# A decoder layer on one core: engine orders in the attention loop, roots by logarithm and exponential, and both joints rearranged

## The chip, the core and the metric

The kernel runs on one core of a Trainium2 chip. The core has TensorE (PE: matmuls and transposes, with its weight loads shown apart as PEld), VectorE (DVE), ScalarE (ACT), GpSimd (POOL), and SyncE (SP), which here only issues DMAs. Each engine works through its own instructions in order and waits on semaphores for the others. The metric is the device time of one execution in microseconds. The kernel before takes 967.76 us, the median of three runs (966.3 to 969.13).

## The reference

All of it is float32: 4096 tokens (16 sequences of 256) of width 256. There are three parts, each followed by a layer norm of x plus its result.

```python
# 1: "attention" against 1024 fixed rows, squared relu instead of softmax (4 heads of 64)
p = jnp.square(jax.nn.relu(jnp.einsum('bhtd,sd->bhts', q, k)))     # q from layernorm(x)*g+b
out = residual + jnp.einsum('bhts,sd->bhtd', p, v)
x = _layernorm(x + out)
# 2: cross attention, 16 heads of 16, with a bias from clipped differences of frac
D = jnp.clip(frac[:, None, :] - frac[:, :, None], -0.2, 0.2)
attn = gamma*logits + delta*(alpha_pos*max(D, 0) + alpha_neg*min(D, 0))
x = _layernorm(x + (softmax(attn) @ V) @ Wo.T + bo)
# 3: top-1 of 8 experts, a shared inner matrix plus a rank-4 part of the expert
inter = relu(x @ wi_W.T + wi_b + lora(x, expert))
x = _layernorm(x + inter @ wo_W.T + wo_b)
```

The root that this case is about is the `rsqrt(var + 1e-5)` of the layer norms, one for each row.

## The kernel before

The order of the work is written out by hand (`manual_schedule`): each engine gets its instructions in the order of the program text. There are three stages and two joints between them.

**First stage** (lines 872 to 953): eight blocks of 512 tokens. For each block and each of eight pieces, `scores` multiplies with the fixed rows, ScalarE applies relu, VectorE squares, and `values` accumulates into two banks. `keep` (331) brings these two banks together: ScalarE copies both, GpSimd adds. `turn_out` (337) turns the result back and forms y = 2x + out on VectorE; `measure_out`, `scaling` and `norm_out` give the normalized rows in `hid`. Slots between the pieces hold the clips of the frac differences (`clips`, `slots`, 859 to 863).

**Second stage** (964 to 1036): 64 groups, four for each of 16 sequences (a batch), each group with four heads (g = 0 to 3). Iteration n works on three groups at once. For group n (`now`): `logits` (592), sixteen matmuls on top of the seeds; `maxima` (606) on VectorE, which adds the negative bias, writes t and keeps the row maxima; `subtract` (617), one half on GpSimd and one on VectorE. For group n+1 (`nxt`): `negative` (571, 576) on GpSimd and ScalarE; `positive` (583), the seed, which ScalarE writes into the bank of PSUM that the logits then add to. It can only be written when the maxima have read that bank. For group n-1 (`last`): `turned(g)` (631), four transposes of t, and `exps(g)` (638), the exponential out of PSUM. For group n-2 (`older`): `attend` (647) and `keep` (655), which copies the finished pair of groups to `raw`; after the second pair, `gather` (502) issues nine DMAs, `sums` and eight pieces of `v`.

Beside that, `pieces(n)` (670) hands out a large piece of matmuls by n modulo 4: 0 the next batch's `queries`, 1 the batch-before-last's `project`, 2 the next `keys`, 3 the next `vals`. Each is a generator of two steps: matmuls into a bank of `tile_b`, then the eviction, on VectorE (on ScalarE for queries). `keys` ends with eight DMAs into `kM`, the four of i=0 first; `logits` of the first and third group of a batch read i=0, of the second and fourth i=1. With n modulo 4 = 2 comes `invert` (519): a reciprocal on VectorE, one DMA `rows` to DRAM, then eight DMAs `invs` back, broadcast. With 3 come the transposes of a later batch's hidden rows (`turned`, 409) and its context; with 0 the `divide` (537), which reads `invs`. All these DMAs are issued on SyncE's queue.

`tile_b` (49) gives the banks for transposes and large pieces: in the second and third stage every third tile comes from the pool psV and the others from the two banks of psB, so the same bank comes round every third tile.

**Third stage** (1038 to 1092): for each block of 512 tokens `norm`, `turn` (707), `gates` (720), `route` (735, the expert's mask), `turn_um` (767), `inner` (778), `lora` (796), `outer` (815), `add` and `store` (835).

`inv_std` (194) gives a row's root everywhere: Sqrt on ScalarE, then a reciprocal on VectorE. In the second stage ScalarE's order in an iteration is: `negative`, `positive(0)`, `positive(1)`, `exps(0)`, `positive(2)`, `exps(1)`, `positive(3)`, `exps(2)`, `exps(3)`. VectorE's is: `maxima`, `subtract`, then the evictions.

Of the kernel before, what the change touches and what calls it, by code (L numbers as in the profile page):

```python
# [14 lines left out]
P = 128  # L15
# [6 lines left out]
def tile_decoder_layer(ctx: ExitStack, tc: tile.TileContext, a: dict, out: bass.AP):  # L22
# [62 lines left out]
    root = const.tile([P, 1], FP, name="root")  # L85
    nc.scalar.activation(root, epst, AF.Sqrt)
# [107 lines left out]
    def inv_std(mv, n):  # L194

        sd = small.tile([P, n], FP, tag="sd", name="sd")
        nc.scalar.activation(sd, mv[:, :, 1], AF.Sqrt, bias=epst)
        rs = small.tile([P, n], FP, tag="rs", name="rs")
        nc.vector.reciprocal(rs, sd)
        return rs  # L200
# [25 lines left out]
    if True:  # L226
# [14 lines left out]
        class Block:  # L241
# [89 lines left out]
            def keep(self, c):  # L331
                half = p1.tile([P, 512], FP, tag="half", bufs=1, name="half")
                nc.scalar.copy(self.oT[:, c, :], self.acc[0])
# [3 lines left out]
            def turn_out(self, jj):  # L337
# [3 lines left out]
                for j in range(2):  # L341
                    for c in range(CC):
# [4 lines left out]
                        )  # L347
                nc.vector.scalar_tensor_tensor(
# [23 lines left out]
    if True:  # L372
# [184 lines left out]
        class Group:  # L557
# [59 lines left out]
            def subtract(self):  # L617
                for g, eng in ((0, nc.gpsimd), (2, nc.vector)):
# [36 lines left out]
            def keep(self):  # L655
                batch = self.batch
                if self.i == 1:
                    if self.o == 0:
                        batch.raw = pm.tile([P, 2, 512], FP, tag="raw", name="raw")
                    if self.o == 0:  # L660
                        nc.vector.tensor_copy(batch.raw[:, self.o, :], batch.av)
                    else:
                        nc.scalar.copy(batch.raw[:, self.o, :], batch.av)
                        batch.gather()
# [25 lines left out]
    if True:  # L690
        out_view = out.rearrange("(b j p) c -> b p j c", j=4, p=P)

        class Block:
# [3 lines left out]
            def norm(self):  # L697
                tb = self.tb
                mv = small.tile([P, 4, 2], FP, tag="mv", name="mv")
                for j in range(4):  # L700
                    row_stats(hid[:, 4 * tb + j, :], mv[:, j, :])
                rs = inv_std(mv, 4)
                self.x2 = tile_x()
                for j in range(4):
                    normed(self.x2[:, j, :], hid[:, 4 * tb + j, :], mv[:, j, 0:1], rs[:, j : j + 1])

            def turn(self):
                self.xT = tile_xt()
                for c in range(CC):
# [5 lines left out]
                    nc.vector.tensor_copy(self.xT[:, c, :], ps)  # L715
# [136 lines left out]
    with tc.manual_schedule():  # L852
# [7 lines left out]
        slots = [(1, (5, 6, 7)), *((tb, (0, 3, 5, 6, 7)) for tb in range(2, 5))]  # L860
# [11 lines left out]
        for tb in range(NB):  # L872
# [6 lines left out]
            if tb > 0:  # L879
                last = rows_in[tb - 1]  # L880
                steps[1] += [lambda: last.turn_out(0), lambda: last.turn_out(1)]
# [77 lines left out]
        block.keep(1)  # L959
# [3 lines left out]

        for n in range(N + 2):
# [4 lines left out]
            if n == 0:  # L969
                small_piece = batches[1].turned()  # L970
# [50 lines left out]
            if n == N:  # L1021
                block.gates()
            if n % 4 == 0:
# [143 lines left out]
```

## Time and profile before

| | |
|---|---|
| median of three runs | 967.76 us |
| the profiled execution | 968.68 us, its span 966.9 us |
| first stage, to the first logits | 268.35 us |
| logits of group 8, 60, 63 start | 328.88, 655.17, 674.06 us |
| steady batch of four groups | 24.95 us |
| first `inner` of the third stage starts | 691.59 us |
| block of the third stage, steady | 32.6 us (738.06 to 770.69) |
| busy PE, DVE, ACT, POOL | 911.5, 708.4, 585.3, 413.6 us |
| activation table loads on ACT | 7, 1283 ns each |

Lines of a timeline read: start in us, length in us, engine, line of the kernel, operation, out<-in, the shapes, how many instructions were merged (x8), and in brackets the idle time of the engine before it with what ended that. SPq is SyncE's queue issuing a DMA. A busy PE is not PE at its peak: matmuls are pipelined, and a matmul that is held up shows longer or starts later.

### The profile page before, as it was taken

What the parts mean: (1) busy time and instruction counts of PE and PEld (TensorE: products, weight loads), DVE (VectorE), ACT (ScalarE), POOL (GpSimd) and SP (SyncE); (2) the same over time, 40 slices, a digit from 0 to 9 for tenths busy, and PEclk for the clock granted to TensorE, in tenths of its full rate; (3) what the DMA queues carried; (4) which work ended last, traced back from release to release, by engine and by line L of the source; (5) the groups of instructions that cost most, each with busy time, mean ns of one, the idle gap of its engine ahead of it and who ended that gap; (6) DMA issues with size and microseconds to landing.
All of it is one profiled execution on the core that took longest, in us unless ns stands there. A gap on an engine that the chain in (4) does not pass through costs nothing.

```text
span 966.9 us, 19117 instructions
## 1 busy us (share of the span) xinstructions
PE 911.5 (94%) x6910; PEld 545.7 (56%) x6910; DVE 708.4 (73%) x1909; ACT 585.3 (61%) x956; POOL 413.6 (43%) x352
## 2 busy tenths in 40 slices
PE   5999999999978999999999999998889999999997
PEld 2333333333345676777676777775446656565656
DVE  4789999999877888888889888888543534453424
ACT  4757776778679888999898999998311010101010
POOL 1102211323466787888888888887211101100100
PEclk9999999999989999999999999999989999999999
DMA  6312221122001222222222222221100000000001
GB/s 171 107 39 77 69 66 64 61 67 66 23 1 45 67 51 62 61 65 63 68 64 69 65 68 67 67 65 35 31 5 1 23 22 1 23 22 22 0 22 44
DMA packets 50526, 48.54 MB, mean 50 GB/s; under 512 B 15616, under 2 KB 40704, under 8 KB 50432
## 3 DMA queue, kind: packets, MB, share of 16 engines
q1 hardware_dynamic: 49712, 46.53, 17.0%
q8 instruction: 55, 0.90, 0.4%
q10 hardware_dynamic: 720, 0.79, 0.3%
q14 instruction: 39, 0.32, 0.1%
HBM read 26.84 MB, written 11.80 MB: 40 GB/s over the span
## 4 chain that ended last, share of the span: by engine, by line
PE 52%; DVE 8%; ACT 3%; issue 2%; SPq 1%; DMA 1%; ACTq 0%; DVEq 0%
PE ps_l L788 12%; PE ps_v L818 10%; PE ps_b L631 7%; PE ps_l L592 6%; PE ps_v L647 4%; DVE t L606 3%; DVE t L621 2%; PE ps_b L442 2%; PE ps_b L544 2%; PE ps_l L800 2%; PE ps_b L422 2%; PE ps_b L818 1%; ACT ps_l L583 1%; ACT pT L638 1%; PE ps_b L712 1%
## 5 line engine op out<-in xcount | busy, mean ns | idle before, releaser
L571 POOL TENSOR_SCALAR neg<-dneg,aneg,delta 128x512 f32<-128x512 f32 x192 | 214.0, 1124 | 0.0
L606 DVE CUSTOM_DVE_ANT_0 t<-ps_l,neg 128x256 f32<-128x256 f32 x512 | 181.4, 420 | 40.8 <-PE ps_l L592 34.9
L583 ACT ACTIVATE ps_l<-dpos,apos_d 128x512 f32<-128x512 f32 x256 | 175.9, 693 | 36.4 <-DVE mx L606 23.6
L313 DVE TENSOR_TENSOR pr<-r 128x1024 f32<-128x1024 f32 x128 | 160.7, 1295 | 24.1 <-ACT r L311 23.8
L311 ACT ACTIVATE r<-ps_a 128x1024 f32<-128x1024 f32 x128 | 126.4, 1023 | 68.4 <-PE ps_a L303 42.3
L631 PE MATMUL ps_b<-ident,t 128*128 128x128 f32 x1024 | 144.4, 281 | 13.3 <-ACT pT L638 12.3
L621 POOL TENSOR_TENSOR t<-t,mx 128x1024 f32<-128x1024 f32 x64 | 121.2, 1893 | 80.2 <-DVE mx L606 70.2
L638 ACT ACTIVATE pT<-ps_b 128x512 f32<-128x512 f32 x256 | 144.5, 595 | 3.5 <-PE ps_b L631 2.9
L631 PEld LDWEIGHTS ps_b<-ident,t 128*128 128x128 f32 x1024 | 113.5, 141 | 56.2 <-ACT pT L638 20.5
L323 PE MATMUL ps_v<-pr,vv 64*64 64x512 f32 x1024 | 124.6, 595 | 4.1 <-DVE pr L313 3.6
L303 PE MATMUL ps_a<-xnT,kT 64*64 64x512 f32 x1024 | 123.6, 599 | 0.3 <-ACT r L311 0.3
L788 PE MATMUL ps_l<-xt,wi 128*128 128x512 f32 x256 | 114.6, 601 | 0.0
L621 DVE TENSOR_TENSOR t<-t,mx 128x1024 f32<-128x1024 f32 x64 | 111.9, 1748 | 2.2
L718 POOL TENSOR_TENSOR x<-x,wofb 128x256 f32<-128x256 f32 x32 | 22.7, 739 | 201.2 <-PE ps_b L712 201.2
L818 PE MATMUL ps_v<-wof,hT 128*128 128x256 f32 x448 | 101.4, 383 | 0.0
L807 ACT ACTIVATE hT<-ps_l,wib 128x512 f32<-128x512 f32 x32 | 20.2, 684 | 122.5 <-PE ps_l L800 122.5
L818 PEld LDWEIGHTS ps_v<-wof,hT 128*128 128x128 f32 x448 | 83.7, 190 | 18.8 <-issue 8.4
L335 POOL TENSOR_TENSOR xt<-xt,half 128x512 f32<-128x512 f32 x16 | 24.9, 1558 | 151.1 <-ACT half L334 151.1
L811 DVE TENSOR_SCALAR hT<-ps_l,wib 128x512 f32<-128x512 f32 x32 | 22.5, 746 | 90.2 <-PE ps_l L800 90.2
L323 PEld LDWEIGHTS ps_v<-pr,vv 64*64 64x64 f32 x1024 | 37.2, 132 | 77.9 <-issue 39.7
L788 PEld LDWEIGHTS ps_l<-xt,wi 128*128 128x128 f32 x256 | 48.4, 194 | 54.9 <-issue 54.6
L592 PE MATMUL ps_l<-kM,qT 32*128 32x256 f32 x1024 | 77.0, 406 | 1.2 <-ACT ps_l L583 1.2
(105 smaller groups left out, 1052.2 us busy)
## 6 DMA issues: line engine op xcount, KB each, us to landing
cT<-in_ctxT SPq DMA_DIRECT2D x16, 256.0 KB
kM<-keys SPq DMA_DIRECT2D x128, 32.0 KB
v<-raw SPq DMA_DIRECT2D x128, 32.0 KB
invs<-rows SPq DMA_DIRECT2D x128, 32.0 KB
x<-in_x SPq DMA_DIRECT2D x7, 512.0 KB
away<-dneg SPq DMA_DIRECT2D x14, 256.0 KB
away<-dpos SPq DMA_DIRECT2D x14, 256.0 KB
dneg<-away SPq DMA_DIRECT2D x14, 256.0 KB
```

Of the source, the lines that this page charges most:

```text
L311: nc.scalar.activation(r, sc, AF.Relu)
L313: nc.vector.tensor_tensor(pr, r, r, ALU.mult)
L323: nc.tensor.matmul(self.acc[k][64 * h : 64 * h + 64, :], lhsT=vv[64 * k : 64 * k + 64, hf, 64 * q : 64 * q + 64], rhs=pr[64 * k : 64 * k + ...
L571: nc.gpsimd.tensor_scalar(self.neg[:, g], self.batch.dneg, aneg[:, h : h + 1], delta, ALU.mult, ALU.mult,)
L583: nc.scalar.activation(banks[g], self.batch.dpos.rearrange("p j k -> p (j k)"), AF.Copy, scale=apos_d[:, h : h + 1],)
L592: nc.tensor.matmul(banks[g][:, j * S : (j + 1) * S], lhsT=self.batch.qT[rows, self.o, j * P : (j + 1) * P], rhs=self.batch.kM[rows, self.i ...
L606: nc.vector.tensor_tensor_reduce(out=self.t[:, g, j, :], in0=banks[g][:, j * S : (j + 1) * S], in1=self.neg[:, g, j, :], scale=1.0, scalar ...
L621: eng.tensor_tensor(rows, rows, top.to_broadcast([P, 4, S]), ALU.subtract)
L631: nc.tensor.transpose(ps[:, k * S + j * P : k * S + (j + 1) * P], self.t[:, g, j, k * P : (k + 1) * P], ident,)
L638: nc.scalar.activation(self.pT[:, g, :], self.ps[g], AF.Exp)
L788: nc.tensor.matmul(banks[g], lhsT=wi[:, c, f * P : (f + 1) * P], rhs=self.xT[:, c, :], start=(c == 0), stop=False,)
L818: nc.tensor.matmul(ps[:, at * C : (at + 1) * C], lhsT=self.hT[f][:, j * P : (j + 1) * P], rhs=wof[:, f, :], start=(f == 0), stop=(f == FC ...
```

## The change

- **Roots.** `inv_std` takes Ln and then Exp(-0.5 ln) on ScalarE as a first guess and one Newton step, three small operations, on VectorE. The table set that holds both functions is asked for at the start, instead of a first Sqrt.
- **ScalarE's order** in an iteration of the second stage: all four `positive` come ahead of `exps(1)`.
- **VectorE's order**: `keep` and the second step of the large piece come ahead of `subtract`, except where n modulo 4 is 0 and in iteration 1 (there the second step of the large piece stays behind `exps(3)`). `keep` always copies on VectorE.
- **`invert`** comes ahead of the large piece `keys` of the same iteration.
- **First joint**: the last `keep` of the first stage adds on VectorE out of PSUM; in iteration 0 the transposes of batch 1, `vals` of batch 0 and both `turn_out` are issued between the logits and the maxima, both halves of `subtract` go to GpSimd, `queries` of batch 1 move to iteration 1. The last block's row statistics are taken in iterations 1 to 4, its root in 5, its `norm_out` in 8 to 11.
- **Second joint**: the first block of the third stage is measured in iterations 58 to 61, normalized on ScalarE in 63 (`begin`), turned there with copies on ScalarE, its gates and route taken in iteration 64; after the loop `norm` of the second block follows `inner(0)` and `turn_um` of the first, ahead of `invert` of the last batch.
- One clip in each of three blocks of the first stage moves from piece 3 to piece 0.

```diff
-    root = const.tile([P, 1], FP, name="root")
-    nc.scalar.activation(root, epst, AF.Sqrt)
+    nc.scalar.preload_act_table_set("natural_log_exp_and_others")
...
     def inv_std(mv, n):
 
-        sd = small.tile([P, n], FP, tag="sd", name="sd")
-        nc.scalar.activation(sd, mv[:, :, 1], AF.Sqrt, bias=epst)
+        ln = small.tile([P, n], FP, tag="ln", name="ln")
+        nc.scalar.activation(ln, mv[:, :, 1], AF.Ln, bias=epst)
+        near = small.tile([P, n], FP, tag="near", name="near")
+        nc.scalar.activation(near, ln, AF.Exp, scale=-0.5)
+
+        t = small.tile([P, n], FP, tag="sd", name="sd")
+        nc.vector.scalar_tensor_tensor(t, mv[:, :, 1], EPS, near, ALU.add, ALU.mult)
+        nc.vector.scalar_tensor_tensor(t, t, -0.5, near, ALU.mult, ALU.mult)
         rs = small.tile([P, n], FP, tag="rs", name="rs")
-        nc.vector.reciprocal(rs, sd)
+        nc.vector.scalar_tensor_tensor(rs, t, 1.5, near, ALU.add, ALU.mult)
         return rs
...
-            def keep(self, c):
+            def keep(self, c, last=False):
+                nc.scalar.copy(self.oT[:, c, :], self.acc[0])
+                if last:
+                    nc.vector.tensor_tensor(self.oT[:, c, :], self.oT[:, c, :], self.acc[1], ALU.add)
+                    return
                 half = p1.tile([P, 512], FP, tag="half", bufs=1, name="half")
-                nc.scalar.copy(self.oT[:, c, :], self.acc[0])
                 nc.scalar.copy(half, self.acc[1])
                 nc.gpsimd.tensor_tensor(self.oT[:, c, :], self.oT[:, c, :], half, ALU.add)
...
                             ident,
                         )
+                yield
                 nc.vector.scalar_tensor_tensor(
...
-            def subtract(self):
-                for g, eng in ((0, nc.gpsimd), (2, nc.vector)):
+            def subtract(self, halves):
+                for g, eng in zip((0, 2), halves):
...
                     if self.o == 0:
                         batch.raw = pm.tile([P, 2, 512], FP, tag="raw", name="raw")
-                    if self.o == 0:
-                        nc.vector.tensor_copy(batch.raw[:, self.o, :], batch.av)
-                    else:
-                        nc.scalar.copy(batch.raw[:, self.o, :], batch.av)
+                    nc.vector.tensor_copy(batch.raw[:, self.o, :], batch.av)
+                    if self.o == 1:
                         batch.gather()
...
+            def measure(self, j):
+                if j == 0:
+                    self.mv = small.tile([P, 4, 2], FP, tag="mvh", name="mv")
+                row_stats(hid[:, 4 * self.tb + j, :], self.mv[:, j, :])
+
+            def begin(self):
+
+                by = scaling(self.mv, 4)
+                self.x2 = tile_x()
+                for j in range(4):
+                    scaled(self.x2[:, j, :], hid[:, 4 * self.tb + j, :], by, j)
+
+            def turn(self, copy=nc.vector.tensor_copy):
...
-                    nc.vector.tensor_copy(self.xT[:, c, :], ps)
+                    copy(self.xT[:, c, :], ps)
...
-        slots = [(1, (5, 6, 7)), *((tb, (0, 3, 5, 6, 7)) for tb in range(2, 5))]
+        slots = [(1, (5, 6, 7)), *((tb, (0, 0, 5, 6, 7)) for tb in range(2, 5))]
...
-                steps[1] += [lambda: last.turn_out(0), lambda: last.turn_out(1)]
+                for jj in range(2):
+                    steps[1].append(lambda jj=jj: [*last.turn_out(jj)])
...
-        block.keep(1)
+        block.keep(1, last=True)
         only.close()
         turns.append(0)
         pm = ctx.enter_context(tc.tile_pool(name="pm", bufs=2))
 
+        rest = rows_in[NB - 1]
+        begun = rows_out[0]
+        rest.mv = const.tile([P, 4, 2], FP, name="mv_rest")
         for n in range(N + 2):
             now, nxt, last, older = (
                 groups[n + d] if 0 <= n + d < N else None for d in (0, 1, -1, -2)
             )
             large_piece, small_piece, more = pieces(n)
-            if n == 0:
-                small_piece = batches[1].turned()
+
+            if n < 2:
+                large_piece = batches[1].queries() if n == 1 else None
             if n % 4 == 3 and n // 4 + 2 < B:
                 batches[n // 4 + 2].reload()
             if now:
                 now.logits()
-            if n == 0:
-                step(early[3])
             if older:
                 older.attend()
-            if n == 0:
-                step(small_piece)
-                step(small_piece)
             if nxt:
                 nxt.negative()
+            if n == 0:
+                turn, outs = batches[1].turned(), [rest.turn_out(jj) for jj in range(2)]
+                for piece in (turn, early[3], *outs, turn):
+                    step(piece)
             if now:
                 now.maxima()
             if nxt:
                 nxt.positive(0)
                 nxt.positive(1)
+            if n == N - 1:
+                begun.begin()
             if last:
                 last.turned(0)
                 last.exps(0)
+                last.turned(1)
             if nxt:
                 nxt.positive(2)
+                nxt.positive(3)
             if last:
-                last.turned(1)
                 last.exps(1)
-            if nxt:
-                nxt.positive(3)
+            if older:
+                older.keep()
+            if n == 0:
+                for piece in (outs[0], early[3], outs[1]):
+                    step(piece)
+            if n % 4 == 2:
+                for extra in more:
+                    if extra:
+                        extra()
+            step(large_piece)
+            late = n % 4 == 0 or n == 1
+            if not late:
+                step(large_piece)
+            if n == N - 1:
+                begun.turn(nc.scalar.copy)
+            if n == N:
+                begun.gates()
             if now:
-                now.subtract()
-            if n == 0:
-                step(early[3])
-            if older and older.o == 1:
-                older.keep()
-            step(large_piece)
-            if n % 4 > 0:
-                step(large_piece)
-            if older and older.o == 0:
-                older.keep()
-            if n < 2:
-                if n == 0:
-                    rows_in[NB - 1].mv = small.tile([P, 4, 2], FP, tag="mv", name="mv")
-                rows_in[NB - 1].turn_out(n)
-                rows_in[NB - 1].measure_out(n)
-            if n == N:
-                block.turn()
+                now.subtract((nc.gpsimd, nc.gpsimd if n == 0 else nc.vector))
             if last:
                 for g in range(2, 4):
                     last.turned(g)
                     last.exps(g)
-            if n == N:
-                block.gates()
-            if n % 4 == 0:
+            if late:
                 step(large_piece)
             step(small_piece)
             step(small_piece)
-            for extra in more:
-                if extra:
-                    extra()
-            if n == 2:
-                by[NB] = scaling(rows_in[NB - 1].mv, 4)
-            if 4 <= n < 8:
-                rows_in[NB - 1].norm_out(by[NB], n - 4, n - 4, nc.vector)
-            if n == N - 1:
-                block = rows_out[0]
-                block.norm()
+            if n == N:
+                begun.route()
+            if n % 4 != 2:
+                for extra in more:
+                    if extra:
+                        extra()
+            if 0 < n < 5:
+                row_stats(rest.y[:, n - 1, :], rest.mv[:, n - 1, :])
+            if n == 5:
+                by[NB] = scaling(rest.mv, 4)
+            if 8 <= n < 12:
+                rest.norm_out(by[NB], n - 8, n - 8, nc.vector)
+            if N - 6 <= n < N - 2:
+                begun.measure(n - (N - 6))
 
         end = batches[B - 1]
         add = end.project()
-        block.route()
-        block.inner(0)
+        begun.inner(0)
+        begun.turn_um()
+        rows_out[1].norm()
         end.invert()
-        block.turn_um()
         for tb in range(NB + 1):
             now = rows_out[tb] if tb < NB else None
             nxt = rows_out[tb + 1] if tb + 1 < NB else None
@@ -1051,7 +1079,7 @@
                 if tb == 1:
                     now.turn_um()
                 now.lora(0)
-            if nxt:
+            if nxt and last:
```

More of the change, by code (lines that the diff above doesn't have):

```diff
@@ L697, in norm @@
             def norm(self):
-                tb = self.tb
-                mv = small.tile([P, 4, 2], FP, tag="mv", name="mv")
                 for j in range(4):
-                    row_stats(hid[:, 4 * tb + j, :], mv[:, j, :])
-                rs = inv_std(mv, 4)
+                    self.measure(j)
+                rs = inv_std(self.mv, 4)
                 self.x2 = tile_x()
                 for j in range(4):
-                    normed(self.x2[:, j, :], hid[:, 4 * tb + j, :], mv[:, j, 0:1], rs[:, j : j + 1])
-            def turn(self):
+                    normed(
+                        self.x2[:, j, :], hid[:, 4 * self.tb + j, :], self.mv[:, j, 0:1],
+                        rs[:, j : j + 1],
+                    )
+            def measure(self, j):
[8 more added lines that the diff above has]
+            def turn(self, copy=nc.vector.tensor_copy):
                 self.xT = tile_xt()
```

## The prediction, made before the changed kernel was seen running

> **What bounds the kernel now.** I read the table of busy time by stretch first, then the timelines of one steady stretch engine by engine, then the chain that ended last, then the waits. Columns of the first table: stretch, PE, weight loads, DVE, ACT, POOL busy (instructions), granted clock, DMA share, GB/s.
>
> ```profile
> 425.00:450.00 25.00, 24.30 (x236) 17.88 (x228) 22.36 (x76) 22.63 (x40) 20.93 (x17) 1.00 0.24 66
> 275.00:300.00 25.00, 18.39 (x144) 12.54 (x144) 20.16 (x68) 19.80 (x31) 16.83 (x14) 0.86 0.07 16
> 700.00:720.00 20.00, 15.26 (x54) 7.24 (x51) 7.97 (x20) 4.33 (x7) 2.77 (x4) 0.83 0.04 9
> 740.00:940.00 200.00, 200.00 (x812) 124.95 (x814) 83.91 (x250) 22.85 (x47) 14.46 (x21) 1.00 0.05 16
> ```
>
> The attention loop (64 groups, 268 to 680) has four engines at 84 to 97%; the feed-forward stage is TensorE alone, with no gap for 200 us; the two joints (275 to 300, 680 to 720) leave TensorE idle and at a lower clock. In the steady loop a batch of four groups takes 24.95 us: logits (L592) start at 380.35, 386.14, 392.05, 398.15 and 405.30, so 5.79, 5.91, 6.10 and 7.15 us.
>
> What sets a group's time is read from ScalarE and TensorE in one group:
>
> ```profile
> 407.47 1.38 ACT L583 ACTIVATE ps_l<-dpos,apos_d 128x512 f32<-128x512 f32 x2 [0.85 <-DVE mx L606]
> 408.78 0.58 ACT L638 ACTIVATE pT<-ps_b 128x512 f32<-128x512 f32 x1
> 409.26 0.68 ACT L583 ACTIVATE ps_l<-dpos,apos_d 128x512 f32<-128x512 f32 x1
> 409.87 0.58 ACT L638 ACTIVATE pT<-ps_b 128x512 f32<-128x512 f32 x1
> 410.35 0.69 ACT L583 ACTIVATE ps_l<-dpos,apos_d 128x512 f32<-128x512 f32 x1
> ```
> ```profile
> 408.31 1.89 PE L422 MATMUL ps_b<-xT,wq 128*128 128x256 f32 x8
> 410.04 1.13 PE L631 MATMUL ps_b<-ident,t 128*128 128x128 f32 x8
> 411.10 1.15 PE L592 MATMUL ps_l<-kM,qT 32*128 32x256 f32 x16
> ```
>
> The loop closes on itself: logits at 405.30, first maximum 1.29 later, first seed (L583) at 2.17, then seed, exponential, seed, exponential (409.87, ends 410.46), seed. The eight transposes at 410.04 are those of g=2 and g=3. tile_b rotates over three banks and an iteration takes five tiles (g0, g1, the large piece, g2, g3), so g3 takes the bank of g1: its first transpose starts at 410.51, 0.05 after the second exponential ends, and the next logits 0.59 after that. The fourth seed (ends 411.04) is ready at the same moment. So both ends of that chain are tight.
>
> The DMA queue of SyncE in the same batch (the third group's work starts at 392.05):
>
> ```profile
> 392.53 0.61 SPq L506 DMA_DIRECT2D sums<-raw  x1
> 393.19 5.13 SPq L514 DMA_DIRECT2D v<-raw  x8
> 398.81 5.49 SPq L458 DMA_DIRECT2D kM<-keys  x8
> 404.39 0.53 SPq L524 DMA_DIRECT2D rows<-inv  x1
> 406.02 3.60 SPq L530 DMA_DIRECT2D invs<-rows  x8
> ```
>
> Key rows go first; the first four, for i=0, are needed by the logits at 405.30. invs waits on the queue for rows to land (1.63 after its issue).
>
> And the idle time of TensorE at the joints, with what ended it:
>
> ```profile
> 282.66 2.22 PE L631 MATMUL ps_b<-ident,t 128*128 128x128 f32 x8 [4.33 <-ACT pT L638]
> 705.62 2.21 PE L712 MATMUL ps_b<-ident,x 128*128 128x128 f32 x8 [4.74 <-DVE x L203]
> ```
>
> **The change, part by part.** Signs: plus is slower.
>
> *Seeds ahead of the second exponential.* Seeds end earlier, but TensorE has g3's transposes ahead of the next logits, and these wait for the exponential, now one seed later. Back-to-back seeds and a seed before an exponential are 0.61 apart (2.51 for four at 273.04, less 0.69, over three). A group's loop becomes 5.80 + 0.61 = 6.41. The fourth group adds the hidden transposes (L409, four at 0.11): 6.85, without today's 0.70 idle behind vaug (L472), since VectorE's evictions go first. A batch: 3 x 6.41 + 6.85 = 26.08 against 24.95, +1.13; over the 13 batches from group 8 to 60: +14.7. Before had 326.3 us there against 13 x 24.95 = 324.4, the rest being late invs (L537 waits); these go: -1.9. Bounds: 0 if the wait were covered, +0.7 a group if the first spacing counts in full.
>
> *Evictions ahead of the subtraction.* Maxima end at 4.17 in a group; the large piece ends on TensorE at 4.9; keys take 0.79 more, the subtraction 1.74: 7.5, just below the 7.7 at which the next maxima start (6.41 + 1.29). Cost nothing while the group lasts 6.41; if it lasted 5.8, VectorE would set 6.2 in the third group. raw (L663, 0.61 on ScalarE every fourth group) becomes a VectorE copy of 0.68 in the time VectorE waits for the piece; attend's stretched 1.40 at 393.20 goes, off the path.
>
> *invert ahead of keys, on SyncE's queue.* In the third group rows and invs are now issued before the key rows. raw ends at 4.85 of the second group; nine gather DMAs take 5.8 to 6.1 (392.53 to 398.33, 417.49 to 423.62): queue free at 4.3 to 4.6 of the third group; reciprocal ends 4.51, rows at 4.6, invs 6.25 to 9.9, key rows from 9.95, 0.635 apart, the fourth at 11.85 (a slow issue of 1.03 makes it 12.3). Landing is not a row of its own for kM; rows land in 1.6 and the chain of waits has 1.94 and 2.81 for invs after the last issue; the semaphore times put kM at 2.0 to 2.6 from issue. I take 2.05: 13.9 to 14.4, against logits of the next batch at 6.41 + 6.85 = 13.26. Wait 0.7 to 1.15, taken 0.9: 13 x 0.9 = +11.7. Bounds: 0 (landing 1.4) and 1.6 (landing 2.8). dneg, dpos, cT behind them are needed a batch later.
>
> *Roots by Ln and Exp.* sd is 0.30 and rs 0.18; now two activations and three dependent VectorE operations about 0.22 apart (the chain L744 to L756 has that pitch). Ln is not in the trace: between root's 0.20 and 0.30 plus a load of 1.28. Taken 0.30: +0.3 and +0.48, 0.78 each; with the bounds 0.5 to 3.3. Twice at the start (before the first transposes at 9.11 and 10.64): +1.5. Once at the end (chain from 961.94): +0.8. The others lie under TensorE; in the first stage (DVE 93 to 95%) a clip moves out of the crowded piece 3, 0 net, -1 to +2.
>
> Six of seven table loads go (1283 ns each); what that is worth is inside the joints below, as only there does a transpose wait behind one. The Trainium skill, page "ScalarE: Activation LUTs", section "What ACT_TABLE_LOAD costs", gives about 2.66 us for a switch, with a drain; in this trace the exponential ends at 293.02, the load runs 293.05 to 294.33 and sd starts at 294.34, so no drain shows. By the page the three loads of the first joint would give up to 4.1 us more than I count.
>
> *First joint.* Maxima of group 0 start at 269.85 (behind VectorE's own add) instead of 270.94 (behind the POOL add L335). Then logits, vals and transposes run without the 4.33 gap and the half clock after it: group 1 5.2 after group 0, then 6.41, 6.41, 6.85 and a batch of 26.98, with 0.5 for extra row statistics: 52.3 against 60.5 (268.35 to 328.88): -8.2. norm_out moves to groups 8 to 11, where VectorE waits for ScalarE's scaling behind the last exponential, some 0.4 each, and four row statistics at groups 58 to 61 spill 0.2 to 0.5: +2.5 in all. Groups 60 to 63: +0.9.
>
> *Second joint.* In group 63 begin() puts the roots' end behind the maxima on VectorE (5.0) and four scalings ahead of the exponentials on ScalarE (to 7.1), so TensorE idles about 4 us and half clock is likely: inner(0) starts some 19 us after the last logits, against 17.5. Then turn of block 1 no longer waits 4.74, but its Ln stands behind umT on ScalarE and its copies behind divide, which waits for invs: gates of block 1 at about 39.2 against 42.6: -3.4 (bounds +2 and -7).
>
> Sum: 1.5 - 8.2 + 14.7 - 1.9 + 11.7 + 2.5 + 0.9 - 3.4 + 0.8 = **+18.6**. The profiled execution took 968.68 with a span of 966.9; 985.5 of span, 987.3 with what lies around it, and 0.9 less at the median of 967.76: **986**.
>
> **Rivals.** *Key rows in time* (landing under 1.4, or the gather shorter): -12.6 with the one at group 8: 974. For it: the spread of landings; against: 20 us of queue in series from raw to the fourth key row. *Only the queue is felt* (g3 not held by the second exponential): a batch is 5.65 + 20.1 = 25.8: about 970, no change. Against: 0.05 us between that exponential and the transpose. *Both covered, faster*: the seeds start the next logits 0.6 earlier, groups take 5.65, 6.05, 6.2 and 6.2 (TensorE and VectorE bound), 24.1 a batch: 13 x (24.1 - 24.95) - 1.9 = -13.0, joint one -9.5, the rest as above: 948. It decides if g3's wait for g1's bank exceeds nothing, that is under 0.1 us a group, and the key rows wait under 0.1. For it: TensorE's own work is only 23 us a batch. *The table stays split*: Ln and Exp in two sets, two loads a root: 2.6 x 3 on the path and some in the loop, 996 to 1000; against: nothing else than Ln, Exp, Relu, Identity and Copy is left to switch for.
>
> **Chances.** Forecast 986 (own range 976 to 998): 0.52. Key rows in time, 974: 0.17. Only the queue, 970: 0.08. Both covered, 948: 0.20. Split table: 0.03. Range 955 to 1000: below lies most of the fourth case, about 0.16. A measurement of this kernel tells some 0.3% (2.9 us) from no change: faster 0.21, same 0.08, slower 0.71.
>
> **What would show it.** Logits 6.4 apart in the first three groups of a batch and about 13.9 to 14.3 from the third group to the next batch; g3's transpose straight behind the second exponential; logits of a new batch released by a DMA of kM; one table load; no 4.33 and no 4.74 gap; a gap near 4 us in group 63. Logits 5.7 apart, or 12.4 over the last two groups, and the forecast is wrong.

## The result and the profile after

The changed kernel takes **980.29 us** (median of four runs, 977.81 to 984.95) against 968.39 for the kernel before, measured beside it: a ratio of 1.0132, 95% interval 1.0091 to 1.0173. It is slower by 11.9 us, four times the 2.9 us that the prediction took as the least that can be told from no change. The profiled execution took 980.28 with a span of 978.5.

The starts of the logits cut both spans at the same places (us):

| stretch | before | after | difference | forecast |
|---|---|---|---|---|
| to the logits of group 0 | 268.35 | 266.75 | -1.6 | +1.5 |
| group 0 to 8 (first joint) | 60.53 | 52.33 | -8.2 | -8.2 |
| group 8 to 60 (13 batches) | 326.29 | 350.83 | +24.5 | +27.0 |
| group 60 to 63 | 18.89 | 18.17 | -0.7 | +0.9 |
| group 63 to the end | 292.84 | 290.42 | -2.4 | -2.6 |
| span | 966.9 | 978.5 | +11.6 | +18.6 |

The busy time by stretch of the changed kernel (stretch, PE, weight loads, DVE, ACT, POOL busy with their instructions, granted clock, DMA share, GB/s):

```profile
277.00:301.00 24.00, 22.01 (x218) 16.11 (x219) 19.15 (x74) 21.04 (x38) 19.45 (x17) 1.00 0.15 45
425.00:450.00 25.00, 23.44 (x214) 16.23 (x213) 18.85 (x64) 20.06 (x36) 19.24 (x16) 1.00 0.23 61
688.00:712.00 24.00, 18.77 (x132) 10.84 (x131) 12.33 (x44) 10.03 (x22) 4.84 (x6) 1.00 0.10 21
```

In these stretches of the two joints the clock is now full (0.86 and 0.83 before); later in the first joint, from 311.75 to 315.17, it is once at half. The loop is the other way round: in 425 to 450 TensorE, VectorE, ScalarE and GpSimd are all less busy than before, VectorE by 3.5 us of 25. So none of them has become the bound; a chain of waits has. The timeline of TensorE in the last two groups of one batch and into the next:

```profile
452.54 0.60 PE L640 MATMUL ps_b<-ident,t 128*128 128x128 f32 x4
453.62 0.66 PE L640 MATMUL ps_b<-ident,t 128*128 128x128 f32 x4 [0.48 <-ACT pT L647]
454.11 0.60 PE L418 MATMUL ps_b<-ident,hid 128*128 128x128 f32 x4
454.64 0.70 PE L601 MATMUL ps_l<-kM,qT 32*128 32x256 f32 x4
455.56 1.32 PE L601 MATMUL ps_l<-kM,qT 32*128 32x256 f32 x12 [0.21 <-DMA kM<-keys]
```

ScalarE at the same time:

```profile
451.28 0.58 ACT L647 ACTIVATE pT<-ps_b 128x512 f32<-128x512 f32 x1
451.76 1.29 ACT L592 ACTIVATE ps_l<-dpos,apos_d 128x512 f32<-128x512 f32 x2
452.99 1.07 ACT L647 ACTIVATE pT<-ps_b 128x512 f32<-128x512 f32 x2
```

The first exponential ends at 451.86, then come two seeds, and only then the second exponential (452.99, two merged, the first of them over by about 453.57). The transposes of the fourth head (453.62) wait for just that one, and the logits stand behind them. So the second, third and fourth group of a batch take 6.41, 6.41 and 6.84 us. The second wait is in the last line: four of the sixteen matmuls of the new batch's logits go out at 454.64, the other twelve wait for key rows until 455.56. The wait lies inside the logits, so it shows as a longer first group: 7.13 us (median of the 13 batches) instead of 6.41. SyncE's queue says why the rows are late:

```profile
439.76 0.62 SPq L515 DMA_DIRECT2D sums<-raw  x1
440.43 5.11 SPq L523 DMA_DIRECT2D v<-raw  x8
445.83 0.34 SPq L533 DMA_DIRECT2D rows<-inv  x1
447.31 3.59 SPq L539 DMA_DIRECT2D invs<-rows  x8
451.01 5.59 SPq L467 DMA_DIRECT2D kM<-keys  x8
```

The key rows are now last in the row, from 451.01; the fourth is issued at about 452.9 and the logits that wait go on at 455.56. In all, over most of the loop (waits of the changed kernel from group 8 on: who waits for whom, us, times, longest):

```profile
PEld ps_b L640 <- ACT pT L647: 36.2, 53, 1.3
PE ps_b L640 <- ACT pT L647: 22.4, 42, 1.1
PEld ps_l L601 <- DMA kM<-keys: 7.1, 21, 0.8
```

TensorE's weight loads stand about five times as long for the exponential as for the key rows; before, the first of these three waits was 6.9 us and the last did not appear. In the second joint the changed kernel's TensorE has these stops:

```profile
693.76 0.33 PE L732 MATMUL ps_b<-ident,x 128*128 128x128 f32 x1 [1.51 <-ACT x L242]
700.82 1.09 PE L640 MATMUL ps_b<-ident,t 128*128 128x128 f32 x8 [1.63 <-POOL t L630]
707.18 1.96 PE L553 MATMUL ps_b<-wo,oT 128*128 128x256 f32 x8 [1.44 <-DVE oT L546]
708.98 7.03 PE L808 MATMUL ps_l<-xt,wi 128*128 128x512 f32 x16
718.69 1.65 PE L732 MATMUL ps_b<-ident,x 128*128 128x128 f32 x8 [0.43 <-DVE x L208]
```

Three stops near 1.5 us, with the clock at 1.00 throughout; the 4.74 of before is now the 0.43 in the last line.

### The profile page after: what moved, and what is told of

It reads as the page before. It is cut to its first block, busy times and chain, and to the rows that moved or that the text cites. A ratio compares the mean times of both kernels' runs of the same rounds, so it can differ in the third digit from the quotient of the medians.

```text
span 978.5 us, 19202 instructions
## 1 busy us (share of the span) xinstructions
PE 921.3 (94%) x6910; PEld 550.8 (56%) x6910; DVE 704.2 (72%) x1980; ACT 584.5 (60%) x968; POOL 419.0 (43%) x352
## 4 chain that ended last, share of the span: by engine, by line
PE 52%; ACT 24%; DVE 15%; issue 6%; DMA 2%; SPq 0%; POOL 0%; ACTq 0%; DVEq 0%; POOLq 0%
ACT ps_l L592 13%; PE ps_l L808 11%; PE ps_v L838 10%; ACT pT L647 8%; DVE pr L318 7%; PE ps_l L601 6%; PE ps_a L308 6%; PE ps_v L328 6%; PE ps_b L640 5%; DVE t L615 2%; PE ps_l L820 2%; PE ps_b L838 1%; ACT qT L441 1%; DVE st L190 1%; DVE y L357 1%
## 5 line engine op out<-in xcount | busy, mean ns | idle before, releaser
L592 ACT ACTIVATE ps_l<-dpos,apos_d 128x512 f32<-128x512 f32 x256 | 171.0, 686 | 52.5 <-DVE mx L615 39.9
L640 PE MATMUL ps_b<-ident,t 128*128 128x128 f32 x1024 | 149.6, 280 | 31.1 <-ACT pT L647 28.3
L318 DVE TENSOR_TENSOR pr<-r 128x1024 f32<-128x1024 f32 x128 | 158.2, 1276 | 17.1 <-ACT r L316 16.7
L630 POOL TENSOR_TENSOR t<-t,mx 128x1024 f32<-128x1024 f32 x65 | 124.0, 1909 | 94.5 <-DVE mx L615 85.8
L808 PE MATMUL ps_l<-xt,wi 128*128 128x512 f32 x256 | 112.5, 592 | 0.0
L838 PEld LDWEIGHTS ps_v<-wof,hT 128*128 128x128 f32 x448 | 83.5, 190 | 18.9 <-issue 8.4
L630 DVE TENSOR_TENSOR t<-t,mx 128x1024 f32<-128x1024 f32 x63 | 93.2, 1479 | 0.6
L601 PE MATMUL ps_l<-kM,qT 32*128 32x256 f32 x1024 | 91.5, 407 | 0.6 <-DMA kM<-keys 0.6
L308 PEld LDWEIGHTS ps_a<-xnT,kT 64*64 64x64 f32 x1024 | 38.2, 134 | 68.4 <-issue 56.7
```

Source lines behind the costliest of these rows:

```text
L308: nc.tensor.matmul(sc[64 * k : 64 * k + 64, h, :], lhsT=kT[64 * h : 64 * h + 64, q, hf * P + 64 * k : hf * P + 64 * k + 64], rhs=self.xnT[ ...
L318: nc.vector.tensor_tensor(pr, r, r, ALU.mult)
L592: nc.scalar.activation(banks[g], self.batch.dpos.rearrange("p j k -> p (j k)"), AF.Copy, scale=apos_d[:, h : h + 1],)
L601: nc.tensor.matmul(banks[g][:, j * S : (j + 1) * S], lhsT=self.batch.qT[rows, self.o, j * P : (j + 1) * P], rhs=self.batch.kM[rows, self.i ...
L630: eng.tensor_tensor(rows, rows, top.to_broadcast([P, 4, S]), ALU.subtract)
L640: nc.tensor.transpose(ps[:, k * S + j * P : k * S + (j + 1) * P], self.t[:, g, j, k * P : (k + 1) * P], ident,)
```

## The experiments

Each kernel was timed against the kernel before, which took 966.89 us beside the first four, 967.13 beside the next four and 967.39 beside the last three. The first four start from the changed kernel, the next five from the kernel before, the last two from the best of the first four.

### From the changed kernel: seeds and invert, each and both put back

**Seeds back**: `turned(1)`, `exps(1)` ahead of `positive(3)` again, all else as changed.

```diff
                 last.exps(0)
-                last.turned(1)
             if nxt:
                 nxt.positive(2)
-                nxt.positive(3)
             if last:
+                last.turned(1)
                 last.exps(1)
+            if nxt:
+                nxt.positive(3)
```

> The changed kernel with ScalarE's old order of seeds and exponentials; all else as changed. My theory (two chains: the second exponential behind four seeds, and the key rows behind invs on SyncE's queue): the groups fall from 6.41 to 5.8 to 6.2 us, but the queue's chain from raw to the key rows (20.6 us from the second group's logits) then sets the batch, so a batch falls only from 27.0 to about 26.4, and the first logits of a batch wait about 1.5 to 2 us for kM. 13 batches x 0.6 plus some 4 us in the groups outside them: 968 us. Rival (seeds cost nothing, something else slowed the loop): 980. Rival (seeds alone are the cause): 962 or less, with no longer wait for kM.

Measured: 995.56 us (991.48 to 999.88), ratio 1.0299 (1.0264 to 1.0334). A miss by 28 us, and on the wrong side of the changed kernel: putting the suspected loss back made it 15 us *slower*. The second and third group of a batch do go back to 5.80, but from group 8 to 60 the first takes 7.4 to 10.9 and the fourth 6.7 to 8.1 (medians 9.24 and 7.27; 28.5 a batch). The timeline of this kernel's TensorE where a new batch begins:

```profile
487.46 3.06 PE L601 MATMUL ps_l<-kM,qT 32*128 32x256 f32 x16 [0.99 <-DMA kM<-keys]
490.45 1.73 PE L656 MATMUL ps_v<-pT,vaug 128*32 128x256 f32 x16
492.11 1.97 PE L640 MATMUL ps_b<-ident,t 128*128 128x128 f32 x8
...
496.70 1.15 PE L601 MATMUL ps_l<-kM,qT 32*128 32x256 f32 x16
```

Its weight loads in those logits:

```profile
487.46 0.29 PEld L601 LDWEIGHTS ps_l<-kM,qT 32*128 32x128 f32 x2 [1.23 <-DMA kM<-keys]
488.06 0.29 PEld L601 LDWEIGHTS ps_l<-kM,qT 32*128 32x128 f32 x2 [0.31 <-DMA kM<-keys]
488.73 0.29 PEld L601 LDWEIGHTS ps_l<-kM,qT 32*128 32x128 f32 x2 [0.38 <-DMA kM<-keys]
489.39 0.72 PEld L601 LDWEIGHTS ps_l<-kM,qT 32*128 32x128 f32 x10 [0.37 <-issue]
```

Its busy time by stretch (the number after POOL's count is the clock):

```profile
487.00:490.00 3.00, 2.54 (x15) 1.46 (x16) 0.00 (x0) 1.00 (x2) 1.21 (x2) 1.00 0.21 51
490.00:493.00 3.00, 3.00 (x26) 1.56 (x22) 2.71 (x15) 1.38 (x2) 1.07 (x1) 0.62 0.52 139
493.00:496.00 3.00, 3.00 (x17) 2.75 (x16) 2.47 (x4) 2.27 (x4) 3.00 (x2) 0.81 0.47 155
```

The late key rows cost three times over: TensorE stands 0.99 us; the logits then take 3.06 us instead of 1.15, as they go out in pairs that wait three more times, for 0.31, 0.38 and 0.37, twice for a DMA of key rows by the profile (+1.9); and the clock falls to 0.62 behind that, so attend takes 1.73 instead of 1.07 and the transposes 1.97 instead of 1.09 (+1.5). The group is 9.24 long, which is 5.80 and these last two. The queue does not get shorter when the groups do: from `raw` of one batch to the fourth key row it is one chain of DMAs. In the changed kernel the later exponentials hide most of that chain: the second, third and fourth group last 19.7 us together there, and 18.4 with both parts back.

**invert back**: `invert` behind the large piece and the small pieces again, seeds as changed.

```diff
-            if n % 4 == 2:
-                for extra in more:
-                    if extra:
-                        extra()
             step(large_piece)
...
-            if n % 4 != 2:
-                for extra in more:
-                    if extra:
-                        extra()
+            for extra in more:
+                if extra:
+                    extra()
```

> The changed kernel with invert behind keys again, seeds still ahead. My theory: groups stay 6.41, 6.41, 6.41, 6.85, the wait for kM goes, a batch is 26.1 instead of 27.0: 14 x 0.9 = 12.6 less, 968 us, if invs still land before divide (I reckon 24.7 against 25.6 us after the second group's logits). Rival (the late kM is hidden by something else late): 979 to 980.

Measured: 967.70 us (967.0 to 969.53, ten runs), ratio 1.0011 (0.9999 to 1.0024): as expected. Groups take 6.41, 6.41, 6.40 and 6.84, a batch 26.06, and no wait for key rows is left among the larger ones. So the move of `invert` costs 12.6 us in the changed kernel, 9.5 of it in the 13 batches from group 8 to 60.

**Both back**: the two edits together.

> The changed kernel with both the seeds and invert put back; VectorE's evictions stay ahead of the subtraction, roots and joints as changed. My theory: groups of 5.8, 6.05, 6.2 (VectorE: piece, eviction, subtraction) and 6.25, a batch of 24.3 to 24.5, late invs perhaps 0.1 to 0.3 a batch: 13 x 2.5 + 3.5 less than the changed kernel, 944 us (941 to 949), faster than both kernels. Rival (the chains only add, the new order of VectorE gives nothing over the old batch of 24.95): 950 or more.

Measured: 940.95 us (940.24 to 941.73), ratio 0.9736 (0.972 to 0.9753): faster than both kernels, and just below the expected range. A batch takes 24.17 (5.80, 5.91, 5.80, 6.67). With the first two experiments and the changed kernel that makes a square (us):

| | invert behind keys | invert ahead of keys |
|---|---|---|
| seeds in their old order | 940.95 | 995.56 |
| seeds ahead | 967.70 | 980.29 |

Seeds ahead cost 26.8 us in the left column and *gain* 15.3 in the right one. `invert` ahead costs 54.6 in the upper row and 12.6 in the lower.

**Three back**: in addition, the copies to `raw` and the large piece's second step behind VectorE's subtraction again.

```diff
-            if older:
-                older.keep()
...
-            step(large_piece)
             late = n % 4 == 0 or n == 1
-            if not late:
-                step(large_piece)
...
                 now.subtract((nc.gpsimd, nc.gpsimd if n == 0 else nc.vector))
+            if older and older.o == 1:
+                older.keep()
+            step(large_piece)
+            if not late:
+                step(large_piece)
+            if older and older.o == 0:
+                older.keep()
```

> As the run before it, and the evictions behind the subtraction again (raw copied by VectorE in both cases, its place as before the change). My theory: groups of 5.8, 5.8, 5.8 and 7.15, the 0.7 us idle behind vaug is back in the fourth group, the hold of 0.4 us by ScalarE's copy of raw is gone: a batch of 24.55, 945 us, within 2 us of the run before it. Rival (evictions ahead are worth the whole idle time): 9 us slower than the run before it, 953.

Measured: 956.78 us (956.03 to 957.09), ratio 0.9896 (0.9881 to 0.9911). The expected 945 is missed, the rival is nearer. The waits of this kernel in the loop:

```profile
DVE oT L546 <- DMA invs<-rows: 11.8, 13, 1.5
PEld ps_b L418 <- DVE vaug L481: 11.2, 12, 0.9
```

With the evictions ahead the second is gone, and the first is 3.2 us in 5 waits over the same stretch. The second line is the idle behind `vaug`: the fourth group is 7.15 against 6.67. The first is the late `invs`: keys evicted behind the subtraction are issued 6.76 us into the third group instead of 5.9, and `invs` behind them come too late for the divide; in 7 of the last 12 batches the second group is then 6.46 or longer instead of 5.91. So this place of the evictions is worth 15.8 us here. By the profiled executions 9.8 lie in the 13 batches, which these two groups make up, 4.0 in groups 60 to 63 and 1.8 ahead of group 8.

### From the kernel before: each part alone

**invert alone** ahead of `keys`, behind the copy to `raw` and VectorE's subtraction.

> The kernel before with one part alone: invert ahead of keys. My theory: raw is copied by ScalarE at 6.4 us of the second group, gather ends 6.4 of the third, key rows go out from 11.7 and the fourth lands at 15.7 against logits at 13.25: a batch 2.4 longer, 14 times, less some 3 us of late invs: 998 us, with waits for kM at each batch's first logits. Rival (the queue has room): 965 to 968.

Measured: 1037.78 us (1033.21 to 1038.66), ratio 1.0724 (1.0698 to 1.075). The direction is right, the size is missed by 40 us. It is the first experiment again, with later evictions ahead of the queue: later batches of 29.8 to 31.6. TensorE at the start of a batch of this kernel:

```profile
510.19 4.00 PE L592 MATMUL ps_l<-kM,qT 32*128 32x256 f32 x16 [0.37 <-DMA kM<-keys]
514.13 1.93 PE L647 MATMUL ps_v<-pT,vaug 128*32 128x256 f32 x16
515.99 1.97 PE L631 MATMUL ps_b<-ident,t 128*128 128x128 f32 x8
```

Logits of 4.00 us, then 1.93 and 1.97 for what takes 1.07 and 1.09. Over the loop the granted clock is 0.90. As in the first experiment, the expectation priced the late rows alone, and not the drawn-out logits and the lower clock.

**Seeds alone**, the first diff the other way round on the kernel before.

> The kernel before with one part alone: all four seeds ahead of the second exponential. My theory: groups of 6.4 to 6.5 us and 6.9 in the fourth, a batch of 26.1 to 26.4: 13 x 1.3 plus 3 in the other groups, less the late invs: 985 us. Rival (the next logits really start 0.6 us earlier): 955 or less.

Measured: 984.72 us (984.42 to 986.54), ratio 1.0189 (1.0173 to 1.0204): as expected. Groups are 6.41, 6.41, 6.41 and 7.15, a batch 26.38.

**The clip alone**: one clip of three blocks from piece 3 to piece 0.

```diff
-        slots = [(1, (5, 6, 7)), *((tb, (0, 3, 5, 6, 7)) for tb in range(2, 5))]
+        slots = [(1, (5, 6, 7)), *((tb, (0, 0, 5, 6, 7)) for tb in range(2, 5))]
```

> The kernel before with one part alone: the clip moved from piece 3 to piece 0 in three blocks of the first stage. The first stage of the changed kernel was 3 us shorter between its first scores and the first logits. If the clip is the cause: 965 us, first logits at 265 to 266 instead of 268.35, and the idle of TensorE behind VectorE's squares in blocks 2 to 4 gone. Rival (the roots or chance are the cause): 968, first logits at 268.

Measured: 964.11 us (962.24 to 965.83, ten runs), ratio 0.9969 (0.9957 to 0.9982). The first logits start at 264.50 instead of 268.35. The kernel before stops TensorE once in each of these three blocks, behind VectorE's squares:

```profile
97.84 1.09 PE L323 MATMUL ps_v<-pr,vv 64*64 64x512 f32 x8 [1.03 <-DVE pr L313]
129.69 1.09 PE L323 MATMUL ps_v<-pr,vv 64*64 64x512 f32 x8 [1.03 <-DVE pr L313]
```

The third, at 161.56, is alike. With the clip moved these stops are gone, and a shorter one stands earlier in each block, where the clip now is:

```profile
88.65 2.23 PE L323 MATMUL ps_v<-pr,vv 64*64 64x512 f32 x16 [0.21 <-DVE pr L313]
119.29 2.22 PE L323 MATMUL ps_v<-pr,vv 64*64 64x512 f32 x16 [0.29 <-DVE pr L313]
```

They are 31.85 apart before and 30.64 here: 1.2 us a block, three blocks.

**The roots alone**: `inv_std` and the table set as changed.

> The kernel before with one part alone: roots by Ln, Exp and a Newton step. My theory: 1.35 us more at the start (as seen in the changed kernel), 0.6 more at the end, one table load instead of seven, which shortens the first joint by 2 to 4 us: 966 to 968. Rival (the loads were the joints' cost): 960 or less. Rival (the roots are the cost): 971 or more. If the first stage gains 3 us here, its gain came from the roots.

Measured: 968.42 us (967.0 to 969.94, ten runs), ratio 1.0016 (1.0006 to 1.0025). The first logits start 1.4 later, group 0 to 8 is 2.3 shorter, the last stretch 1.3 longer: six table loads fewer, and nothing won.

**The evictions alone**: copies to `raw` (always on VectorE) and the large piece's second step ahead of the subtraction.

```diff
+            if older:
+                older.keep()
+            step(large_piece)
+            late = n % 4 == 0 or n == 1
+            if not late:
+                step(large_piece)
             if now:
                 now.subtract()
...
-            if older and older.o == 1:
-                older.keep()
-            step(large_piece)
-            if n % 4 > 0:
-                step(large_piece)
-            if older and older.o == 0:
-                older.keep()
```

> The kernel before with only the third part: raw copies and the second step of the large piece ahead of VectorE's subtraction, raw copied on VectorE always; roots, seeds, invert and both joints as before. Theory (what the pair of runs with and without it in the new kernel showed, 15.8 us, was half made of the new joints and half of this): the 0.70 idle behind vaug in the fourth group and the late invs go, a batch falls from 24.95 to about 24.2, group 8 to 60 from 326.3 to about 317, L60 to L63 falls by about 1: 957 us. Rival: all of the 15.8 belongs to this part: 952. Other rival: the evictions only matter with the earlier seeds away and the new raw copy delays VectorE: 967, no change.

Measured: 953.89 us (951.96 to 956.56), ratio 0.9857 (0.9834 to 0.988), between the two; the interval is about 951 to 956. A batch takes 24.16 (5.80, 5.91, 5.80, 6.66), group 8 to 60 takes 316.0 and 60 to 63 16.2 against 18.9. So this part wins 13.5 us by itself, 10.3 of it in the 13 batches. It is not quite the part that was worth 15.8 above: there VectorE copied `raw` in both kernels, here that copy also moves from ScalarE. In the steady loop three back differs from the kernel before by the engine of that copy alone, and its third group takes 5.80 instead of 6.10; what the copy's place and the large piece's second step each bring was not separated.

### From the best kernel so far

**The second joint**: the kernel with both back, and after the loop:

```diff
         begun.inner(0)
-        begun.turn_um()
-        rows_out[1].norm()
         end.invert()
+        rows_out[1].norm()
+        begun.turn_um()
```

> The kernel with ScalarE's old order of seeds and invert behind keys (941 us), and after the loop the last batch's invert straight behind inner(0), then norm of the second block, then turn_um of the first, in place of turn_um, norm, invert. Theory: the divide waits less for invs and the Ln of the second block no longer stands behind umT on ScalarE, so two stops of 1.4 us and 0.4 us of TensorE shrink: 939, between 938 and 940. Rival: turn_um comes later on VectorE and its transposes stop TensorE as long as before: 941 to 942.

Measured: **938.95 us** (938.36 to 939.99), ratio 0.9702 (0.9684 to 0.9719), the best of all. From the logits of group 63 to the end it takes 289.4 us against 290.9. Of the two stops that were meant to shrink, the 0.43 in front of the second block's transposes is gone, and with it one of 0.40 in front of its gates; the one in front of `project` is not, nor the 0.68 in front of `lora` (this kernel's TensorE):

```profile
667.69 1.97 PE L553 MATMUL ps_b<-wo,oT 128*128 128x256 f32 x8 [1.45 <-DVE oT L546]
...
677.63 1.14 PE L820 MATMUL ps_l<-umT,loraB 32*128 32x512 f32 x8 [0.68 <-ACT umT L796]
678.70 1.09 PE L732 MATMUL ps_b<-ident,x 128*128 128x128 f32 x8
```

So the size came out as expected, and half of the reason given for it was wrong: `project` waits 1.45 us for the divide, as before (1.44).

**The old roots** in the kernel with both back: Sqrt and reciprocal, and their loads.

> The kernel with ScalarE's old order of seeds and invert behind keys (941 us), and in it the old roots again: Sqrt and reciprocal, with their table loads. Theory: the start wins 1.35 and the last root 0.8, the loop nothing, and the loads of 1.28 us that come back at the two joints cost 1 to 4 us together, as ScalarE waits for VectorE there anyway: 941, between 939 and 943. Rival: the roots by logarithm and exponential are what made the joints short, and each load ahead of an exponential stops the transposes and TensorE's clock as well: 946 or more.

Measured: 945.49 us (944.95 to 947.37), ratio 0.9772 (0.9755 to 0.9788): 4.5 us more than with the new roots, a miss of the range and short of the rival's 946. The profiled execution is the slowest of its four, and 7.1 us longer than that of both back (span 945.6 against 938.5). It shows where: to the first logits -0.55, group 0 to 8 +6.3, group 63 to the end +1.9. ScalarE of this kernel, at the root of the last block of the first stage, now inside the loop:

```profile
302.21 1.28 ACT L197 ACT_TABLE_LOAD   x1
303.50 0.30 ACT L197 ACTIVATE sd<-mv_rest,epst 128x4 f32<-128x4 f32 x1
...
306.43 1.28 ACT L642 ACT_TABLE_LOAD   x1
```

and its TensorE behind that:

```profile
308.37 1.09 PE L635 MATMUL ps_b<-ident,t 128*128 128x128 f32 x8 [2.25 <-ACT pT L642]
309.40 2.72 PE L596 MATMUL ps_l<-kM,qT 32*128 32x256 f32 x16
```

The same kernel's busy time by stretch, with the clock third from the end:

```profile
305.00:308.00 3.00, 1.12 (x6) 0.64 (x4) 3.00 (x15) 2.94 (x4) 2.20 (x2) 1.00 0.16 36
...
311.00:314.00 3.00, 3.00 (x23) 1.02 (x19) 2.54 (x15) 1.99 (x3) 0.90 (x1) 0.50 0.23 53
```

Three loads stand in the stretch from group 0 to 8. The first, at 273.07, makes groups 0 to 3 longer by 1.4 us, about its own length. The other two stop TensorE for 2.25, the half clock follows, and groups 4 to 7 are 4.9 us longer, for 2.56 us of loads.

## Why the prediction was right, point by point

The forecast of 986 stands 5.7 us above the 980.29 that were measured, and the reasons that decided its sign held.

- **Seeds ahead of the second exponential**: 6.41 a group and 6.85 in the fourth were forecast; 6.41, 6.41, 6.40 and 6.84 came with invert back, and the last three of these in the changed kernel too. The wait was named correctly (the fourth head's transposes, for the second exponential), and the kernel without the key-row wait shows 26.06 a batch against 26.08. The rival *both covered* fell by this.
- **invert ahead of keys**: 0.9 a batch was taken, out of 0.7 to 1.15. The changed kernel's 350.83 over 13 batches against 341.33 with invert back is 0.73 a batch, 9.5 in all against 11.7. The wait does not lie where the prediction looked for it: from the third group to the next batch it is 13.25 us, and not 13.9 to 14.3, since the logits start in time and wait inside. The rival *key rows in time* was priced at -12.6 for an absent wait; taking the wait away gave -12.6 between the medians, as close as that by luck.
- **Evictions**: "cost nothing" is right beside groups of 6.41. That they bring 13.5 us to the kernel before was not seen: the forecast credits them with the late `invs` (-1.9) and the 0.30 in the fourth group alone. It also held that VectorE would then set 6.2 us in the third group if groups lasted 5.8; with both back the third group takes 5.80.
- **Late norm_out and statistics**: +2.5. With invert back the 13 batches took 341.3 against 13 x 26.06 = 338.8: 2.5. All of it lies in groups 8 to 15; the spill that was counted for groups 58 to 61 does not show in the last batch of these (26.05).
- **Roots**: +1.5 at the start came as +1.35 (the first scores start at 13.66 instead of 12.31). Ln, taken as 0.30, is 0.29 to 0.30.
- **First stage, mis-sized**: the moved clip was taken as "0 net, -1 to +2". It gave -2.95 between the first scores and the first logits, outside these bounds; run alone the clip gave -3.6 over the same stretch. The three stops of 1.03 stood in the trace of before; the table by stretch, read as averages of 93 to 95% on VectorE, hid them.
- **First joint**: -8.2 forecast and measured. Order and roots both have a part in it: in the kernel with both back this stretch is 12.3 shorter than before (48.2 against 60.5), and 6.3 of that are gone with the old roots. Neither joint's new order was run alone.
- **Groups 60 to 63, mis-sized**: +0.9 forecast, -0.7 measured. Evictions ahead shorten this stretch alone by 2.7 (18.9 to 16.2), which was left out.
- **Second joint**: -2.6 forecast, -2.4 measured, though its parts differ: one stop of about 4 us with a half clock was expected, there were three of about 1.5, with the clock at 1.00. `inner(0)` starts 20.9 after the last logits, not 19, and the gates of the second block come 39.5 after them, against 39.2: two errors of 1.9 and 1.6 cancel, so that this term came out is luck.

The 7.0 us between the forecast and the measured span are these: 3.1 to the first logits, 2.5 in the loop, 1.6 in groups 60 to 63, less 0.2 at the end.

What the prediction did not contain is how much its two losses depend on each other. They were added as if each had its own price. By the square above, neither has one. The rival *only the queue is felt* had the queue set the batch with no delay by the exponential, at 25.8 us a batch and 970 in all; the run nearest to it, seeds back, took 28.5 a batch and 995.56. The exponential's delay lengthens the groups and with them the time that the queue has; without it the same queue costs 54.6 us, because the wait then draws out the logits and the clock falls behind it. The sum came out well because the wait was worked out against the *lengthened* batch (13.26 us over its last two groups).

## What to carry to other kernels

Price a change of order against the other parts of the same change, and against the batch as it will then be: two edits that each lose may hide one another, so undoing the one that looks worst can make the kernel slower, and a part that wins (the evictions here) is found only by running it alone. In a loop that is closed by a chain of waits, an instruction put ahead of the one that frees the next buffer costs its whole length in every turn (here one seed, 0.61 us a group). Look for single stops of TensorE that recur, such as the three of 1.03 us, not at averages of busy time.

## What was not expected of the hardware

- The granted clock fell after stops of 2.25 us (old roots: 0.50 in 311 to 314) and, with key rows late, after 0.99 us and logits that waited three more times (0.62 in 490 to 493); it stayed at 1.00 after stops of 1.51, 1.63 and 1.44 in the second joint of the changed kernel. The length of a stop alone does not decide it: in the kernel before, one of 2.37 (from 679.27) left the clock at 1.00, and in the changed kernel one of 1.05 (from 309.59) was followed by 0.50 from 311.75 to 315.17. The Trainium skill, page "TensorE: Matmul & The Clock Gate", section "Why this matters for your kernels", sets the limit at idle gaps of about 3 us between bursts. Here shorter ones were enough in some cases; what decides was not tried.
- A table load took 1.28 us and the next activation began 0.01 later (303.49 to 303.50), as before. What it cost beyond its length came with the slower TensorE afterwards: 1.4 us for one load and 4.9 for two in groups 0 to 7 of the run with the old roots.
